# One run of 40 rows per image in the resident tile of a diagonal LSTM kernel

## The chip, the cores and the metric

The kernel runs on one core of a Trainium2 chip. The metric is device time in microseconds (us) of one execution. The core has TensorE (PE in the profile; PEld is its weight load), VectorE (DVE), ScalarE (ACT), GpSimd (POOL) and SyncE (SP), each with its own instruction queue, and 16 DMA engines.

## The reference, cut to what matters

The input `x` holds 16 images of 128 channels and 64 x 64 pixels in float32. Two layers follow each other, each of the form x + f(groupnorm(x)) with 32 groups of 4 channels. In layer 0, f is an LSTM that runs along the diagonals of the image. Each row of the image is shifted right by its own number, so that a step of the recurrence takes all rows at once, one column each:

```python
xs = skew(x)                       # row i shifted right by i
i_s = einsum('oi,bihw->bohw', w_is, xs) + b_is
def step((h, c), ist):             # over the 127 columns of the skewed image
    h_shift = pad(h)[:, :, :-1]    # the row above
    gates = ist + w_ss[:, :, 0] @ h_shift + w_ss[:, :, 1] @ h + b_ss
    o, f, i = sigmoid(gates[:, :384]) in three parts; g = tanh(gates[:, 384:])
    c = f * c + i * g
    h = o * tanh(c)
x = x + unskew(hs)                 # after _gn(x) on the way in
...
xq = xf @ pre_w.T + pre_b          # layer 1, for each pixel: 128 -> 4
z = _simulate(xq, q_weights)       # a circuit of 4 qubits
x = x + z @ post_w.T + post_b      # 4 -> 128
```

## The kernel before, in words

Channels lie on the 128 partitions. **Stage one** loads all images and takes their statistics. The tile `ring` (L110) stays in SBUF through the whole kernel and has room for 40 of the 64 rows of every image. It is cut into 10 blocks of 4 rows; the block is the outer dimension, then the image, then the 256 values of the 4 rows. So one image's 40 rows lie in ten runs of 1 KB per partition, and one block of all 16 images is one contiguous run. `block(r)` (L136) gives the index of the block that holds row r: rows 0 to 31 lie in blocks 2 to 9, rows 32 to 39 in blocks 0 and 1. `rows(b)` (L244) loads an image in five DMAs of two blocks on SP's queue; `behind(b)` (L252) brings the other 24 rows into small tiles, for the statistics alone. `statistics(b, k)` (L282) is a `bn_stats` on DVE for each 8 rows. Beside it `inv_step` (L187) runs the recurrence of a padding state on PE, ACT and POOL.

**Stage two** is the scan (`step`, L758), 160 steps in an order written out by hand. The rows are worked in two bands of 32 slots: while the first band's last rows finish, the second band's first rows begin, a slot for each row modulo 32. In a step the active slots of all 16 images lie side by side, row pairs in two halves (`q` = 0 and 1). The diagonal of a band is what the active slots read and write in `ring`: one pixel from each row, one column further to the left in each following row. `diagonal(t, band, q, j0, j1)` (L533) gives it in pieces, since rows of one block stand 64 values apart and the blocks 4096: single slots at odd ends, and runs of pairs as one access of four dimensions.

The order of the issue in a step t is:

- `differences` (L615): one subtraction on DVE (L617), and one or two on POOL (L620, L623); PE's products read them.
- `statistics(us)` (L708): on DVE, as many waiting `bn_stats` (L720) for layer 1's norm as fit in the time given. When a block of 4 rows of all 16 images is through, and its rows are among the first 24, the function issues the refill on SP's queue (L727): rows 40 and up of `x` into the same block, 2 MB.
- `residual(t - 1)` (L625): POOL adds the new h to the diagonal of the step before, band 0 and then band 1, `q` = 0 and then 1 (L632). When this completes a block of the first 24 rows, SP stores it to `low` in DRAM (L644), 2 MB. The statistics of that block follow in later steps.
- `normalised(t + 2)` (L561): POOL takes the diagonal of two steps ahead, subtracts the mean (L570) or the upper row (L575), and multiplies with 1/std (L580). PE's input product L589 reads it.
- PE's products with `wsT`, then `w1T` and `w0T` in turns (L768), gate by gate; `w0T` reads POOL's differences. DVE (L783, L835, L843, L846, L853) and ACT (L787, L818, L847) work out the gates and the new state. L853 writes the new h.
- PE's input product for step t + 1 (`gate_ps`, L582).
- POOL copies the last slot for the next band (`edge`, L873).

The tile framework finds which instruction has to wait for which from the address ranges of the accesses. In the scan the order of the instructions on each engine is as written (`manual_schedule`).

**Stage three** is layer 1, image by image: `angles`, `sines`, `squares`, `outputs`, and `finish` (L1057), which adds the result to x on DVE (L1072) and sends 256 KB to the output on SP's queue (L1073). The input is read from `ring`, and for the first 24 rows from tiles that are loaded from `low`. Because 8 rows of an image are two runs of 1 KB in `ring`, `finish` writes the sum to another place in the ring, two neighbouring images' places in a block, so that the DMA reads one run of 2 KB; these belong to images that are done with.

Of the kernel before, what the change touches and what calls it, by code (L numbers as in the profile page):

```python
# [11 lines left out]
F32 = mybir.dt.float32  # L12
# [69 lines left out]
def kernel(  # L82
# [24 lines left out]

    ring = const.tile([P, RING // ROWS, NB, BLOCK], F32, name="ring")  # L110
    NLOW = NH - RING
    NT = NLOW * NW // CHUNK
    low = dram.tile([NB, P, NLOW * NW], F32, name="low")
# [19 lines left out]
    w_out = const.tile([P, 128], F32, name="w_out")  # L133
    b_out = const.tile([P, 1], F32, name="b_out")

    def block(r):  # L136

        return (r + AHEAD if r < SLOTS else r - SLOTS) // ROWS

    def group_mean(psum, v, mean, which, scale):  # L140

# [15 lines left out]
    with ExitStack() as scan:  # L157
# [58 lines left out]
        with ExitStack() as prep:  # L216
# [25 lines left out]
            rests = {}  # L242

            def rows(b):  # L244
                for k in ORDERED:
                    at = (2 * k * ROWS - AHEAD) * NW if k else SLOTS * NW
                    nc.sync.dma_start(
                        out=ring[:, 2 * k : 2 * k + 2, b, :],
                        in_=xv[b, :, at : at + CHUNK].rearrange("c (k n) -> c k n", n=BLOCK),
                    )  # L250

            def behind(b):  # L252
# [27 lines left out]
            nc.gpsimd.memset(cinv[:, 0:1], 0.0)  # L280

            def statistics(b, k):  # L282
                v = ring[:, 2 * k : 2 * k + 2, b, :] if k < 5 else rests[b][k - 5]
                nc.vector.bn_stats(stats[:, b, k, :], v)

            def aggregated(b):
# [85 lines left out]
            for b in range(NB):  # L372
                while b < NB - 1 and done * (NB - 1) < EARLY * (b + 1):
                    inv_step(done, ps_inv)
                    keep(ps_keep, "keep", ring[:, 2, b, 0:P])
# [129 lines left out]
        origin = ring[:, 0, 0, 0:1]  # L505

        def active(t):
            return max(0, t - BAND - NW + 1), min(t + 1, SLOTS)
# [24 lines left out]
        def diagonal(t, band, q, j0, j1):  # L533


            j = j0
            while j < j1:
                odd = (j + AHEAD // 2 * (1 - band)) % 2
                n = 1 if odd or j + 1 == j1 else (j1 - j) // 2 * 2
                r = 2 * j + q + AHEAD * (1 - band)  # L540
                at = r // ROWS * NB * BLOCK + r % ROWS * NW + t - BAND * band - 2 * j - q
                dims = [[BLOCK, NB]]
                if n > 1:
                    dims = [[NB * BLOCK - ROWS, n // 2], [2 * NW - 2, 2]] + dims
                yield j, n, bass.AP(origin.tensor, origin.offset + at, [list(origin.ap[0])] + dims)
                j += n

        def slots(t, band):

            return max(0, t - BAND * band - NW + 1), min(SLOTS, t - BAND * band + 1)  # L550

        def over(v, n):
            if n == 1:
                return v
            return v.unsqueeze(1).unsqueeze(1).to_broadcast([P, n // 2, 2, NB])

        def by_pairs(v, q, j, n):
            v = v[:, q, j * NB : (j + n) * NB]
            return v if n == 1 else v.rearrange("p (k h i) -> p k h i", h=2, i=NB)

        def normalised(t):  # L561

            xn = xns[t % 2]
            for band in range(2):
                s0, s1 = slots(t, band)
                j0, j1 = max(0, s0 - 1 + s0 % 2) // 2, (s1 + 1) // 2
                for j, n, x0 in diagonal(t, band, 0, j0, j1):
                    nc.gpsimd.tensor_sub(by_pairs(xn, 0, j, n), x0, over(mean1, n))  # L570
                j0, j1 = s0 // 2, s1 // 2
                uppers = diagonal(t, band, 0, j0, j1)
                for (j, n, lower), (_, _, upper) in zip(diagonal(t, band, 1, j0, j1), uppers):
                    of = over(mean1, n) if plain(t) else upper
                    nc.gpsimd.tensor_sub(by_pairs(xn, 1, j, n), lower, of)  # L575
# [4 lines left out]
            nc.gpsimd.tensor_mul(v, v, r)  # L580
# [44 lines left out]
        def residual(t, new, engine=nc.gpsimd):  # L625

            for band in range(2):
                s0, s1 = slots(t, band)
                for q in range(2):
                    j0, j1 = (s0 + 1 - q) // 2, (s1 + 1 - q) // 2  # L630
                    for j, n, x1 in diagonal(t, band, q, j0, j1):
                        engine.tensor_add(x1, x1, by_pairs(new, q, j, n))  # L632
# [15 lines left out]


# [58 lines left out]
        def statistics(us):  # L708

            while waiting:  # L710
# [3 lines left out]
                    break  # L714
                waiting.pop(0)
                q = block(4 * g)
                v = ring[:, q, i, :].rearrange("p (r w) -> p r w", w=NW)[:, :, w0:w1]
                if w1 - w0 == NW:
                    v = ring[:, q, i, :]
                nc.vector.bn_stats(stats[:, i, g - FIRST * k, :], v)  # L720
                if i == NB - 1:
                    if g == FIRST - 1:
                        sums.append(early_sums())
                    elif g >= FIRST:
                        sums.append(late_sums(g, k, (w1 - w0) / NW))
                    if 4 * g < NLOW:
                        nc.sync.dma_start(  # L727
                            out=ring[:, q],
                            in_=xv[:, :, (RING + 4 * g) * NW : (RING + 4 * g + 4) * NW].rearrange(
                                "b c n -> c b n"  # L730
                            ),
                        )
# [143 lines left out]
        def low_rows(queue, n, v):  # L876
            b, k = n // NT, n % NT
            of = low[b, :, k * CHUNK : (k + 1) * CHUNK]
            queue.dma_start(out=v, in_=of if len(v.shape) == 2 else of.rearrange("p (k n) -> p k n", n=BLOCK))

        waiting = []
        begin(nc.gpsimd.tensor_copy, cst, 0, cinv, 0)
# [1 line left out]
        with tc.manual_schedule():  # L884
# [23 lines left out]
                add(ps[:, 1], by_one, inner[:, :, h])  # L908
            fill(1)

            v = ring[:, block(NH - ROWS)].rearrange("p i (r w) -> p i r w", w=NW)[:, :, :, NW - STRIP :]
# [64 lines left out]
    def rows_of(b, k):  # L976
        if k < NT:
            return lows[NT * b + k]
        q = block(2 * ROWS * k)
        return ring[:, q : q + 2, b, :]  # L980

    def half(v, c):

        if c is None:
            return v
        return v[:, c] if len(v.shape) == 3 else v[:, c * BLOCK : (c + 1) * BLOCK]

    def bank(pool, name):
        return pool.tile([P, CHUNK], F32, name=name, tag=pool.name)
# [67 lines left out]
    def finish(b, h, po, c=None):  # L1057
        for j in range(4):
            k = 4 * h + j
            v = rows_of(b, k)  # L1060
            x1, y, o = half(v, c), po[j], ov[b, :, k * CHUNK : (k + 1) * CHUNK]
            to = place = v
            if c is not None:
                o, to = o[:, c * BLOCK : (c + 1) * BLOCK], x1
            elif k >= NT:


                q = block(2 * ROWS * k)
                to = ring[:, q, b - 1 : b + 1, :] if b % 2 else ring[:, q + 1, b - 2 : b, :]
                y = y.rearrange("p (k n) -> p k n", n=BLOCK)  # L1070
                place = to.rearrange("p k n -> p (k n)")
            nc.vector.scalar_tensor_tensor(to, y, b_out, x1, ALU.add, ALU.add)  # L1072
            nc.sync.dma_start(out=o, in_=to if c is not None else place)  # L1073
            if c is None or c == 1 and k < NT:
                places.append(place)

    def idle():

# [93 lines left out]
```

## Time and profile before

Three runs took 1411.84, 1413.09 and 1413.08 us, a median of 1413.08. The profile shows one more execution. The page gives its span, and no separate total time for it.

| | |
|---|---|
| span of the profiled execution | 1411.1 us |
| median of the runs shown | 1413.08 us |
| busy: PE, DVE, POOL, ACT | 96%, 69%, 65%, 55% of the span |
| ring loads in stage one | 80 of 256 KB, median 5.6 us to landing |
| stores to `low`, refills | 6 and 6, of 2 MB each, medians 7.5 and 8.3 us |
| POOL's adds to `ring` (L632) | 487, 247.7 us |
| bytes moved by DMA | 107.06 MB |

Times are microseconds unless marked ns. A row of the slices shows the span in 40 parts; a digit is the busy share in tenths. For PEclk it is the clock that PE was granted, in tenths of full speed. A row of the costly groups names line, engine and operation, output and inputs with their shape, the count, then the busy time and the mean ns of one, then the engine's idle time just before, and what ended most of it. A row of the timeline is the start, the duration, the engine, the line and the operation; in brackets the idle time before it and what ended it. A DMA's row gives its issue; the time to landing counts from there.

### The profile page before, as it was taken

How to read it: one execution, taken by the hardware profiler on the slowest of the kernel's cores; microseconds unless marked ns; L12 is line 12 of the kernel's file. 1: busy time of each engine (PE TensorE's matmuls, PEld its weight loads, DVE VectorE, ACT ScalarE, POOL GpSimd, SP SyncE). 2: the span in 40 equal slices, each digit the busy share in tenths (PEclk: the TensorE clock that was granted, in tenths of full speed). 3: DMA queues.
4: the chain of work that ended last, by engine and by line, in shares of the span. 5: the costliest groups of instructions: out<-in, count | busy, mean ns of one | idle time of the engine just before them, and what ended most of it. 6: DMA issues, size and time to landing. Idle time of an engine off the chain costs nothing. (4 is left out here: it accounts for less than half of the span.)

```text
span 1411.1 us, 20316 instructions
## 1 busy us (share of the span) xinstructions
PE 1354.3 (96%) x6046; PEld 966.1 (68%) x6046; DVE 979.7 (69%) x2541; ACT 777.0 (55%) x1852; POOL 921.1 (65%) x1823
## 2 busy tenths in 40 slices
PE   6778999999999999999999999999999999999995
PEld 4658988777777777666677777776666777886332
DVE  7983565566665666787777776666665566876996
ACT  4545666555555555555555555555555566554331
POOL 4226788777777777777788876777777677773300
PEclk9999999999999999999999999999999999999997
DMA  9980000000000000133333100000000000004999
GB/s 326 367 287 2 1 2 0 1 1 1 0 1 1 0 1 1 60 120 120 120 120 120 60 1 1 0 1 1 1 1 0 1 1 1 2 30 143 386 404 350
DMA packets 78925, 107.06 MB, mean 76 GB/s; under 512 B 5552, under 2 KB 53712, under 8 KB 78816
## 3 DMA queue, kind: packets, MB, share of 16 engines
q1 hardware_dynamic: 74176, 94.39, 19.2%
q0 software_dynamic: 3408, 10.58, 2.0%
q8 instruction: 48, 0.79, 0.2%
q10 hardware_dynamic: 1232, 0.80, 0.2%
q14 instruction: 61, 0.50, 0.1%
HBM read 59.61 MB, written 46.14 MB: 75 GB/s over the span
## 5 line engine op out<-in xcount | busy, mean ns | idle before, releaser
L589 PE MATMUL ps<-spare,wxT 128*128 128x512 f32 (+18 forms) x1280 | 480.6, 519 | 0.0
L783 DVE TENSOR_TENSOR ps<-ps,both 128x256 f32<-128x256 f32 (+9 forms) x536 | 219.5, 411 | 304.4 <-PE ps L768 302.6
L787 ACT ACTIVATE ps<-ps,bias 128x512 f32<-128x512 f32 (+23 forms) x480 | 279.4, 583 | 221.7 <-DVE ps L783 185.2
L768 PE MATMUL ps<-spare,w1T 128*128 128x256 f32 (+16 forms) x1272 | 346.6, 354 | 8.8 <-DVE spare L744 4.6
L589 PEld LDWEIGHTS ps<-spare,wxT 128*128 128x128 f32 x1280 | 231.8, 191 | 172.6 <-issue 155.5
L768 PE MATMUL ps<-spare,w0T 128*128 128x256 f32 (+16 forms) x1272 | 343.8, 352 | 0.8 <-POOL spare L623 0.8
L818 ACT COPY both<-ps 128x256 f32<-128x256 f32 (+9 forms) x536 | 189.8, 356 | 181.1 <-PE ps L768 161.4
L632 POOL TENSOR_TENSOR ring<-ring,spare 128x256 f32<-128x256 f32 (+8 forms) x487 | 247.7, 540 | 30.8 <-DVE stats L720 20.7
L768 PEld LDWEIGHTS ps<-spare,w1T 128*128 128x128 f32 x1272 | 230.4, 190 | 35.8 <-DVE spare L853 6.8
L768 PEld LDWEIGHTS ps<-spare,wsT 128*128 128x128 f32 x1088 | 195.5, 190 | 80.5 <-DVE spare L853 29.9
L768 PE MATMUL ps<-spare,wsT 128*128 128x256 f32 (+14 forms) x1088 | 243.8, 366 | 2.4 <-DVE spare L853 1.2
L768 PEld LDWEIGHTS ps<-spare,w0T 128*128 128x128 f32 x1272 | 230.3, 190 | 22.2 <-POOL spare L623 1.0
L580 POOL TENSOR_TENSOR spare<-spare,rstd 128x512 f32<-128x512 f32 (+10 forms) x160 | 171.0, 1069 | 14.8 <-DVE rstd L154 2.3
L575 POOL TENSOR_TENSOR spare<-ring 128x256 f32<-128x256 f32 (+8 forms) x213 | 147.2, 701 | 0.0
L847 ACT ACTIVATE g<-cst 128x256 f32<-128x256 f32 (+20 forms) x320 | 103.2, 369 | 64.2 <-DVE cst L846 63.3
L570 POOL TENSOR_TENSOR spare<-ring,mean 128x16 f32<-128x16 f32 (+8 forms) x247 | 130.9, 540 | 8.3 <-DVE mean L144 7.2
L853 DVE TENSOR_TENSOR spare<-g,ps 128x256 f32<-128x256 f32 (+17 forms) x319 | 105.7, 368 | 43.3 <-ACT g L847 40.8
L623 POOL TENSOR_TENSOR spare<-spare 128x240 f32<-128x240 f32 (+9 forms) x136 | 102.7, 755 | 29.3 <-DVE spare L853 25.5
L787 ACT ACTIVATE g<-ps,bias 128x512 f32<-128x512 f32 (+20 forms) x160 | 97.4, 609 | 26.9 <-DVE ps L783 20.7
L873 POOL COPY spare<-spare 128x16 f32<-128x16 f32 x64 | 21.1, 330 | 134.2 <-DVE spare L853 134.2
L846 DVE TENSOR_TENSOR cst<-cst,ps 128x256 f32<-128x256 f32 (+20 forms) x320 | 104.6, 368 | 5.5
L843 DVE TENSOR_TENSOR ps<-ps,g 128x512 f32<-128x512 f32 (+20 forms) x160 | 95.1, 595 | 19.0 <-ACT g L787 18.8
(370 smaller groups left out, 1097.3 us busy)
## 6 DMA issues: line engine op xcount, KB each, us to landing
out_dram<-ring SPq DMA_DIRECT2D x93, 256.0 KB, 5.3
ring<-in_x_dram SPq DMA_DIRECT2D x80, 256.0 KB, 5.6
low<-ring SPq DMA_DIRECT2D x6, 2048.0 KB, 7.5
ring<-in_x_dram SPq DMA_DIRECT2D x6, 2048.0 KB, 8.3
spare<-in_x_dram SPq DMA_DIRECT2D x27, 256.0 KB, 5.5
rest<-in_x_dram SPq DMA_DIRECT2D x21, 256.0 KB, 5.6
ring<-low POOLq DMA_DIRECT2D x18, 256.0 KB, 6.7
low<-low POOLq DMA_DIRECT2D x14, 256.0 KB, 5.9
```

What stands on the lines that cost most here:

```text
L570: nc.gpsimd.tensor_sub(by_pairs(xn, 0, j, n), x0, over(mean1, n))
L575: nc.gpsimd.tensor_sub(by_pairs(xn, 1, j, n), lower, of)
L580: nc.gpsimd.tensor_mul(v, v, r)
L589: nc.tensor.matmul(ps[g][:, :, a:b], lhsT=wxT[:, g * 128 : (g + 1) * 128], rhs=xns[t % 2][:, :, a:b], start=t > 0, stop=True, skip_group_c ...
L632: engine.tensor_add(x1, x1, by_pairs(new, q, j, n))
L768: nc.tensor.matmul(out, lhsT=w[:, g * 128 : (g + 1) * 128], rhs=rhs, start=False, stop=True, skip_group_check=True,)
L783: nc.vector.tensor_add(v, v, both[g][:, a:b])
L787: nc.scalar.activation(to[:, :, a:w], ps[g][:, :, a:w], FUNC[g], bias=bias[:, g : g + 1])
L818: nc.scalar.copy(both[g][:, a:b], ps[g][:, 0, a:b])
L846: nc.vector.tensor_add(c[:, q], c[:, q], ig[:, q])
L847: nc.scalar.activation(th[:, q, a:w], c[:, q], AF.Tanh)
L853: nc.vector.tensor_mul(new[:, q, a:v], th[:, q, a:v], act[GO][:, q, a:v])
```

## The change

`ring` gets the image as its outer dimension, and each image's 40 rows in one run of 10 KB per partition. `place(r)` is the offset of row r in it, and `block(r)` now gives an access: 4 rows of all 16 images, 16 runs of 1 KB that stand 10 KB apart. A diagonal is then regular from row to row (63 values further for each row, 126 for each pair), so `diagonal` gives a single access of pairs by images, and `residual` and `normalised` issue one instruction where they issued one for each piece. `rows` loads an image in three DMAs: 16 rows, 16 rows, and 8 rows. `finish` writes in place. Refill and store keep their position in the issue order, and what they move.

```diff
-    ring = const.tile([P, RING // ROWS, NB, BLOCK], F32, name="ring")
+    ring = const.tile([P, NB, RING * NW], F32, name="ring")
...
+    def place(r):
+        return (r + AHEAD if r < SLOTS else r - SLOTS) * NW
     def block(r):
-        return (r + AHEAD if r < SLOTS else r - SLOTS) // ROWS
+        return ring[:, :, place(r) : place(r) + BLOCK]
...
             def rows(b):
-                for k in ORDERED:
-                    at = (2 * k * ROWS - AHEAD) * NW if k else SLOTS * NW
+                for r, n in ((0, SLOTS // 2), (SLOTS // 2, SLOTS // 2), (SLOTS, AHEAD)):
                     nc.sync.dma_start(
-                        out=ring[:, 2 * k : 2 * k + 2, b, :],
-                        in_=xv[b, :, at : at + CHUNK].rearrange("c (k n) -> c k n", n=BLOCK),
+                        out=ring[:, b, place(r) : place(r) + n * NW],
+                        in_=xv[b, :, r * NW : (r + n) * NW],
                     )
...
         def diagonal(t, band, q, j0, j1):
-            j = j0
-            while j < j1:
-                odd = (j + AHEAD // 2 * (1 - band)) % 2
-                n = 1 if odd or j + 1 == j1 else (j1 - j) // 2 * 2
-                r = 2 * j + q + AHEAD * (1 - band)
-                at = r // ROWS * NB * BLOCK + r % ROWS * NW + t - BAND * band - 2 * j - q
-                dims = [[BLOCK, NB]]
-                if n > 1:
-                    dims = [[NB * BLOCK - ROWS, n // 2], [2 * NW - 2, 2]] + dims
-                yield j, n, bass.AP(origin.tensor, origin.offset + at, [list(origin.ap[0])] + dims)
-                j += n
+            r = 2 * j0 + q + AHEAD * (1 - band)
+            at = r * NW + t - BAND * band - 2 * j0 - q
+            dims = [[2 * NW - 2, j1 - j0], [RING * NW, NB]]
+            return bass.AP(origin.tensor, origin.offset + at, [list(origin.ap[0])] + dims)
...
                     j0, j1 = (s0 + 1 - q) // 2, (s1 + 1 - q) // 2
-                    for j, n, x1 in diagonal(t, band, q, j0, j1):
-                        engine.tensor_add(x1, x1, by_pairs(new, q, j, n))
+                    if j0 < j1:
+                        x1 = diagonal(t, band, q, j0, j1)
+                        engine.tensor_add(x1, x1, by_pairs(new, q, j0, j1))
...
                             out=low[:, :, 4 * g * NW : (4 * g + 4) * NW].rearrange("b c n -> c b n"),
-                            in_=ring[:, block(4 * g)],
+                            in_=block(4 * g),
...
                 q = block(4 * g)
-                v = ring[:, q, i, :].rearrange("p (r w) -> p r w", w=NW)[:, :, w0:w1]
+                v = q[:, i].rearrange("p (r w) -> p r w", w=NW)[:, :, w0:w1]
...
-                            out=ring[:, q],
+                            out=q,
...
-            to = place = v
+            to = v
...
-            elif k >= NT:
-                q = block(2 * ROWS * k)
-                to = ring[:, q, b - 1 : b + 1, :] if b % 2 else ring[:, q + 1, b - 2 : b, :]
-                y = y.rearrange("p (k n) -> p k n", n=BLOCK)
-                place = to.rearrange("p k n -> p (k n)")
             nc.vector.scalar_tensor_tensor(to, y, b_out, x1, ALU.add, ALU.add)
-            nc.sync.dma_start(out=o, in_=to if c is not None else place)
+            nc.sync.dma_start(out=o, in_=to)
```

The remaining edits follow the new shape: `normalised` loops over no pieces, `statistics` of stage one, `rows_of`, `half` and the strip of the last block read the same elements by the new offsets.

More of the change, by code (lines that the diff above doesn't have):

```diff
@@ L282, in statistics @@
             def statistics(b, k):
-                v = ring[:, 2 * k : 2 * k + 2, b, :] if k < 5 else rests[b][k - 5]
+                v = ring[:, b, k * CHUNK : (k + 1) * CHUNK] if k < 5 else rests[b][k - 5]
                 nc.vector.bn_stats(stats[:, b, k, :], v)
@@ L374 @@
                     inv_step(done, ps_inv)
-                    keep(ps_keep, "keep", ring[:, 2, b, 0:P])
+                    keep(ps_keep, "keep", ring[:, b, CHUNK : CHUNK + P])
                     keep(ps_keep, "keep", wsT[:, 0:P])
@@ L504 @@
         nc.vector.memset(cst[:, :, 0:LEAST], 0.0)
-        origin = ring[:, 0, 0, 0:1]
+        origin = ring[:, 0, 0:1]
         def active(t):
@@ L552, in over, with by_pairs @@
         def over(v, n):
[L553 to L559, printed above, removed]
+            return v.unsqueeze(1).to_broadcast([P, n, NB])
+        def by_pairs(v, q, j0, j1):
+            return v[:, q, j0 * NB : j1 * NB].rearrange("p (j i) -> p j i", i=NB)
         def normalised(t):
@@ L568, in normalised @@
                 j0, j1 = max(0, s0 - 1 + s0 % 2) // 2, (s1 + 1) // 2
-                for j, n, x0 in diagonal(t, band, 0, j0, j1):
-                    nc.gpsimd.tensor_sub(by_pairs(xn, 0, j, n), x0, over(mean1, n))
+                if j0 < j1:
+                    x0 = diagonal(t, band, 0, j0, j1)
+                    nc.gpsimd.tensor_sub(by_pairs(xn, 0, j0, j1), x0, over(mean1, j1 - j0))
                 j0, j1 = s0 // 2, s1 // 2
[L572 to L575, printed above, removed]
+                if j0 < j1:
+                    lower, upper = (diagonal(t, band, q, j0, j1) for q in (1, 0))
+                    of = over(mean1, j1 - j0) if plain(t) else upper
+                    nc.gpsimd.tensor_sub(by_pairs(xn, 1, j0, j1), lower, of)
             a, b = columns(t)
@@ L630, in residual @@
                     j0, j1 = (s0 + 1 - q) // 2, (s1 + 1 - q) // 2
-                    for j, n, x1 in diagonal(t, band, q, j0, j1):
-                        engine.tensor_add(x1, x1, by_pairs(new, q, j, n))
+                    if j0 < j1:
+                        x1 = diagonal(t, band, q, j0, j1)
+                        engine.tensor_add(x1, x1, by_pairs(new, q, j0, j1))
             for g in range(NG2):
@@ L716, in statistics @@
                 q = block(4 * g)
-                v = ring[:, q, i, :].rearrange("p (r w) -> p r w", w=NW)[:, :, w0:w1]
+                v = q[:, i].rearrange("p (r w) -> p r w", w=NW)[:, :, w0:w1]
                 if w1 - w0 == NW:
-                    v = ring[:, q, i, :]
+                    v = q[:, i]
                 nc.vector.bn_stats(stats[:, i, g - FIRST * k, :], v)
@@ L878, in low_rows @@
             of = low[b, :, k * CHUNK : (k + 1) * CHUNK]
-            queue.dma_start(out=v, in_=of if len(v.shape) == 2 else of.rearrange("p (k n) -> p k n", n=BLOCK))
+            queue.dma_start(out=v, in_=of)
         waiting = []
@@ L909 @@
             fill(1)
-            v = ring[:, block(NH - ROWS)].rearrange("p i (r w) -> p i r w", w=NW)[:, :, :, NW - STRIP :]
+            v = block(NH - ROWS).rearrange("p i (r w) -> p i r w", w=NW)[:, :, :, NW - STRIP :]
             d, sq = (work.tile([P, NB, ROWS, STRIP], F32, name=f"strip{i}", tag=f"both{i}") for i in range(2))
@@ L978, in rows_of @@
             return lows[NT * b + k]
-        q = block(2 * ROWS * k)
-        return ring[:, q : q + 2, b, :]
+        at = place(2 * ROWS * k)
+        return ring[:, b, at : at + CHUNK]
     def half(v, c):
@@ L985, in half @@
             return v
-        return v[:, c] if len(v.shape) == 3 else v[:, c * BLOCK : (c + 1) * BLOCK]
+        return v[:, c * BLOCK : (c + 1) * BLOCK]
     def bank(pool, name):
@@ L1061, in finish @@
             x1, y, o = half(v, c), po[j], ov[b, :, k * CHUNK : (k + 1) * CHUNK]
-            to = place = v
+            to = v
             if c is not None:
                 o, to = o[:, c * BLOCK : (c + 1) * BLOCK], x1
-            elif k >= NT:
-                q = block(2 * ROWS * k)
-                to = ring[:, q, b - 1 : b + 1, :] if b % 2 else ring[:, q + 1, b - 2 : b, :]
-                y = y.rearrange("p (k n) -> p k n", n=BLOCK)
-                place = to.rearrange("p k n -> p (k n)")
             nc.vector.scalar_tensor_tensor(to, y, b_out, x1, ALU.add, ALU.add)
-            nc.sync.dma_start(out=o, in_=to if c is not None else place)
+            nc.sync.dma_start(out=o, in_=to)
             if c is None or c == 1 and k < NT:
-                places.append(place)
+                places.append(v)
     def idle():
```

## The prediction

> **What bounds the kernel now.** I read the page from the top: busy shares, slices, costly groups, DMA issues; then the timeline of the one step around the first refill, where the change touches what is late.
>
> ```profile
> PE 1354.3 (96%) x6046; PEld 966.1 (68%) x6046; DVE 979.7 (69%) x2541; ACT 777.0 (55%) x1852; POOL 921.1 (65%) x1823
> ...
> PE   6778999999999999999999999999999999999995
> ...
> POOL 4226788777777777777788876777777677773300
> PEclk9999999999999999999999999999999999999997
> DMA  9980000000000000133333100000000000004999
> ```
>
> Three stages show. In slices 1 to 3 (to about 100 us) the DMA row is full: images load while DVE takes statistics. From 108 to 1283 us PE stands at 9 throughout: the scan. In the last four slices DMA is full again: layer 1 writes out. The scan is 83% of the span and PE has no gaps in it; POOL at 7 or 8 is no bound, it waits for DVE once a step. In the middle the DMA row shows six exchanges of ring rows (store to `low`, refill from `in_x`).
>
> ```profile
> L632 POOL TENSOR_TENSOR ring<-ring,spare 128x256 f32<-128x256 f32 (+8 forms) x487 | 247.7, 540 | 30.8 <-DVE stats L720 20.7
> ...
> L873 POOL COPY spare<-spare 128x16 f32<-128x16 f32 x64 | 21.1, 330 | 134.2 <-DVE spare L853 134.2
> ...
> low<-ring SPq DMA_DIRECT2D x6, 2048.0 KB, 7.5
> ring<-in_x_dram SPq DMA_DIRECT2D x6, 2048.0 KB, 8.3
> ```
>
> The residual add L632 never waits for a DMA, though each refill takes 8.3 us to land. L873 idles 134.2 us over 64 steps, 2.1 us a step: POOL's slack. The timeline of POOL, SP and PE in step 70, where the first refill is issued:
>
> ```profile
> 610.46 0.86 POOL L623 TENSOR_TENSOR spare<-spare 128x240 f32<-128x240 f32 x1
> 611.29 2.34 POOL L632 TENSOR_TENSOR ring<-ring,spare 128x16 f32<-128x16 f32 x7
> 613.59 0.67 POOL L570 TENSOR_TENSOR spare<-ring,mean 128x192 f32<-128x192 f32 x1
> ...
> 615.82 1.27 POOL L580 TENSOR_TENSOR spare<-spare,rstd 128x512 f32<-128x512 f32 x1
> 618.73 0.20 POOL L873 COPY spare<-spare 128x16 f32<-128x16 f32 x1 [1.64 <-DVE spare L853]
> 618.88 0.41 POOL L620 TENSOR_TENSOR spare<-spare,spare 128x16 f32<-128x16 f32 x1
> 619.25 0.69 POOL L623 TENSOR_TENSOR spare<-spare 128x240 f32<-128x240 f32 x1
> ```
>
> ```profile
> 613.59 0.38 SPq L727 DMA_DIRECT2D ring<-in_x_dram  x1
> ```
>
> ```profile
> 621.07 0.59 PE L768 MATMUL ps<-spare,w0T 128*128 128x256 f32 x2
> ```
>
> POOL's order in a step is edge copy, differences for PE, residual, then the normalised diagonal of two steps ahead. The differences end at 619.94 (619.25 + 0.69) and PE's w0T product wants them at 621.07: 1.13 us to spare. The refill is issued at 613.59 and lands at 621.9, when the residual of its own step is long over.
>
> **What the Trainium skill says.** "TensorE: Matmul & The Clock Gate", Part 1: after an idle window of about 3.4 us PE falls to half clock, and regains the full one after about 3.4 us of work. The trace agrees with the half and with the recovery, and is harsher on the idle. Windows (times, total, then PE, PEld, DVE, ACT, POOL busy, granted clock, DMA share, GB/s):
>
> ```profile
> 100.00:101.00 1.00, 0.03 (x1) 0.06 (x1) 0.83 (x2) 0.00 (x0) 0.00 (x0) 1.00 0.00 0
> 103.00:104.00 1.00, 1.00 (x3) 0.48 (x2) 0.78 (x4) 0.98 (x2) 0.00 (x0) 0.50 0.00 0
> ```
>
> PE is idle for some 1.4 us to 101, and from 103 to about 106.4 runs at 0.50. "DMA: Bandwidth & Descriptors" gives one load stream with 4 KiB rows 408.7 GB/s (section on the iDMA fabric); the load phase here, with 1 KB rows in part, shows 362 to 374. "GPSIMD Engine Reference", section 3.1, gives about 2.6 cycles an element plus a dispatch of each instruction; L632's forms agree (256 elements 862 ns, 16 elements 229 ns: 2.6 ns an element and about 0.19 us fixed).
>
> **The change, part by part.**
>
> *Loads.* 80 ring loads become 48, with runs of 4 and 2 KB in place of 1 KB. All loads are 33.6 MB (16 images of 2 MB); at 408.7 instead of 368 GB/s the 21 MB of the ring would take 51.3 instead of 57 us, 5.7 less. But DVE is as full: L284's 128 statistics of 694 ns are 88.8 us, from 13.4 to 100.5, with only 9.4 us of waits for ring loads. The inverse-state chain ends at 94.3, so little more than 5 us can come out of both. Against it: the first load is twice as large, so DVE starts later by up to 1 us, and the weights on ACT's queue share engines with bigger packets. Between −4 and +3; I take −1. At nothing stands SP's shorter issue time, behind loads that fill the engines.
>
> *POOL.* The diagonals become one access each: in the built order L570 falls from 247 to 191 instructions, L575 from 244 to 188, the residual from 487 to 375. That is 224 fewer, each with 0.19 to 0.23 us fixed, 43 to 51 us of POOL. PE covers all of it, since POOL waits 2.1 us a step for DVE: 0. The stride over images becomes 10 KB; no row shows that. Today's strided L632 and contiguous L623 cost the same per element (862 for 256, 801 for 240), so I take no change. It could cost at most what the idle covers without effect; the case beyond is a rival.
>
> *New waits.* A diagonal was several accesses, each within a 4-row block that lay by itself. Now the block of 4 rows (`block`) is a stripe through every image, and a diagonal is one access across many rows and all images. Its address range overlaps that of the block in transfer, although no element is shared, and the built program orders them: the first residual add waits, in six steps, for the refill that the same step's statistics have just sent off, and in six others for the store of the step before. The kernel before has no such wait; there POOL meets the refill only in later steps, when it has landed.
>
> Refill, six times. Behind the waiting add in POOL's queue lie the other residual adds, the normalised diagonal (SP only issues, at 613.59), the next edge copy and the next differences, for which PE's w0T waits. First one: landing 613.59 + 8.3 = 621.9; then residual in fewer pieces 1.9 (the four-piece one at 593.19 took 1.91), normalised 3.5 (613.59 to 617.09), copy and differences 1.2: ready at 628.5 instead of the wanted 621.07, **7.4 us**. The others are issued at 647.27 to 785.08, with w0T wanted 8.95 us later (656.22; the last 794.03): 8.3 + 1.9 + 3.5 + 1.2 − 8.95 = 5.95 each, five times 29.8. Sum **37 us**. PE is the bound in every step around, so nothing makes it up. Ends: an 8.1 or 8.6 landing, shorter late diagonals (the adds shrink to under 10 slots in the band that waits): 30 to 42.
>
> Clock. Each of these stops leaves PE idle 6 to 7 us, so I expect 3.4 us at half clock after it: 1.7 us lost, six times, **10 us**; ends 0 and 20 (the whole recovery counted twice).
>
> Store, six times. It lands 7.5 us after issue (585.55 → 593.1), before the last statistics of that step (596.6), for which the residual now waits as well. That holds POOL 1.7 to 3.5 us; idle of 1.4 to 2.4, pieces saved (0.4 to 1.0) and the 1.13 spare cover it: 0, ends 0 and +4. Statistics wait for POOL in some more places; DVE has idle time every step (L783 302.6 us before it): 0.
>
> *Layer 1 in place.* The writes go out in 2 KB runs either way, DMA at 386 to 404 GB/s sets its end: 0, with L1072's waits for the shifted places gone, and no more than 1 us.
>
> Sum against the profiled execution: 1411.1 − 1 + 37 + 10 = 1457. The page gives its span alone; the runs shown have a median of 1413.08, 2.0 above. So 1459 us.
>
> **Rivals.**
>
> 1. *No clock drop.* The stops happen, but the clock stays: 1459 − 10 = 1449. For it: the stop is short against a step. Against: the 0.50 at 103.
>
> 2. *The wait is covered, the loads win* (the other side). Each add waits at the head of POOL's queue, but the refill is already there when POOL comes to it, because statistics and refill run ahead of the residual; then the load phase's gain of up to 4 is left: 1409 to 1413 on the runs' scale, mostly within reach of faster. It decides the sign where the landing comes within 8.95 − 6.6 = 2.3 us of the issue (0.9 for the first): what PE's need leaves after POOL's 6.6 us of work behind the wait. Against: 8.1 us is the shortest landing of the six, and DVE sends the refill 2.3 us after POOL could begin its residual (611.29 to 613.59).
>
> 3. *POOL becomes the bound.* A full step's ring accesses on POOL are two residual adds of 0.86, L570 0.85 and L575 1.08, 3.65 us; with L580, copy and differences, 2.5 more, it is 6.1 of the step's 8.6. If the 10 KB stride slowed ring accesses by 70%, POOL would fill the step; at twice their time it stands 1.1 us over it, in some 100 steps 110 us: with the stops about 1570. For it: no row has that stride; against: strided and contiguous run alike now.
>
> 4. *The packets do nothing*: DVE sets the load phase and the −1 goes: 1460, within the forecast's spread.
>
> **Chances.** Stops with clock loss 0.66, without 0.20, POOL bound 0.06, covered 0.08. The last is faster (0.06) or the same (0.02). 0.2%, 2.8 us, is about what a measurement here can tell from no change. Range: the low end from rival 1 with the small stops and the good loads (1413 − 4 + 30 = 1439), the high end from the stops' upper end with a clock loss of 20 and the store's 4 (1413 + 3 + 42 + 20 + 4 = 1482). What is left out is the covered case and a slow POOL.
>
> **What would show it.** The waits list should hold POOL's residual waiting for DMA ring<-in_x six times, some 8 to 10 us each, and PE's w0T waiting for POOL's differences six times, about 6 us. Slices 18 to 23 should lose PE's 9 and some of PEclk's. POOL's instruction count should fall by 224 and its busy time by about 45 us; ring loads should number 48. The scan outside 615 to 800 us should keep 8.6 us steps. I am wrong if POOL's residual waits for no DMA; if PE stays full in the middle; or if steps far from the refills grow longer, which means POOL's access rate.

## The result and the profile after

The changed kernel takes 1460.66 us (median of 4 runs, 1459.45 to 1460.85) against 1412.82 us before: ratio 1.0341, interval 1.0327 to 1.0356. The forecast was 1459, slower. The profiled execution has a span of 1458.5 us, 47.4 over the one of before. The page of the kernel after, with the rows that answer to those shown ahead:

```profile
PE 1368.0 (94%) x6046; PEld 974.5 (67%) x6046; DVE 972.0 (67%) x2541; ACT 776.8 (53%) x1852; POOL 887.0 (61%) x1599
...
PE   6788999999999999988888899999999999999995
...
POOL 4226777776677767566556577777777666763310
PEclk9999999999999999999999999999999999999998
DMA  9950000000000000323332200000000000003999
...
L627 POOL TENSOR_TENSOR ring<-ring,spare 128x256 f32<-128x256 f32 (+15 forms) x375 | 231.7, 645 | 103.8 <-DMA ring<-in_x_dram 56.2
...
low<-ring SPq DMA_DIRECT2D x6, 2048.0 KB, 7.5
ring<-in_x_dram SPq DMA_DIRECT2D x6, 2048.0 KB, 8.1
```

PE falls from 9 to 8 in six slices, the ones in which the refills run; elsewhere in the scan it stands as before. POOL has 224 instructions and 34 us of work less, and PE gained nothing by it. L627, the residual, now idles 56.2 us for refills. The waits (engine, line, releaser: us in total, times, longest us) give the two ends of the chain:

```profile
POOL ring L627 <- DMA ring<-in_x_dram: 56.2, 6, 10.0
...
PE ps L763 <- POOL spare L617: 35.1, 7, 6.6
```

Six waits of 9.4 us on POOL become six stops of PE. Here is the first of them in the timeline, on SP, POOL and PE:

```profile
611.14 0.37 SPq L722 DMA_DIRECT2D ring<-in_x_dram  x1
```

```profile
619.53 1.89 POOL L627 TENSOR_TENSOR ring<-ring,spare 128x208 f32<-128x208 f32 x4 [10.04 <-DMA ring<-in_x_dram]
621.38 0.67 POOL L564 TENSOR_TENSOR spare<-ring,mean 128x192 f32<-128x192 f32 x1
...
623.56 1.26 POOL L574 TENSOR_TENSOR spare<-spare,rstd 128x512 f32<-128x512 f32 x1
...
625.10 0.69 POOL L617 TENSOR_TENSOR spare<-spare 128x240 f32<-128x240 f32 x1
```

```profile
618.65 0.59 PE L763 MATMUL ps<-spare,w1T 128*128 128x256 f32 x2
625.84 0.80 PE L763 MATMUL ps<-spare,w0T 128*128 128x256 f32 x1 [6.60 <-POOL spare L617]
```

This refill lands 8.3 us after its issue (the median of the six is 8.1), POOL works off what lay behind the wait for 6.3 us (619.53 to 625.79), and w0T starts at once. After it PE is slow. Windows of the kernel after (columns as ahead):

```profile
622.00:624.00 2.00, 0.00 (x0) 0.00 (x0) 0.00 (x0) 0.00 (x0) 1.92 (x5) 0.59 0.00 0
...
626.00:628.00 2.00, 2.00 (x5) 1.64 (x6) 0.43 (x1) 0.36 (x1) 2.00 (x5) 0.50 0.00 0
...
630.00:632.00 2.00, 2.00 (x8) 1.21 (x7) 1.96 (x4) 1.29 (x3) 1.07 (x1) 1.00 1.05 348
```

The clock falls while PE stands still and is back by 630. In windows of 0.5 us around all six stops, the time of low clock is 3.4 us once and 6.8 us five times, part of it inside the stop; what PE loses while it works is 1.7 to 3.0 us a stop, 13.5 in all. Waiting 34.5 and clock 13.5 make 48.0 of the loss; step by step the stops shift the scan by 49.3 us, so 1.3 us, some 0.2 a stop, are in neither. In these two executions the scan starts 1.3 to 1.7 us earlier than before. That gain is not a fixed amount: the profiled execution of before had half clock from 102.97 to 106.38, and among the eight profiled executions that load and start the scan as the change does the first input product starts between 103.1 and 104.4 us, against 104.5 and 104.6 in two with that of before.

### The profile page after: what moved, and what is told of

Same layout as the page of the kernel before. It is cut to its first block, busy times and chain, and to the rows that moved or that the text cites. A ratio compares the mean times of both kernels' runs of the same rounds, so it can differ in the third digit from the quotient of the medians.

```text
span 1458.5 us, 20029 instructions
## 1 busy us (share of the span) xinstructions
PE 1368.0 (94%) x6046; PEld 974.5 (67%) x6046; DVE 972.0 (67%) x2541; ACT 776.8 (53%) x1852; POOL 887.0 (61%) x1599
## 4 chain that ended last, share of the span: by engine, by line
PE 77%; DVE 4%; DMA 3%; POOL 3%; issue 1%; ACT 1%; DVEq 0%; ACTq 0%; SPq 0%; POOLq 0%
PE ps L763 44%; PE ps L583 26%; DMA ring<-in_x_dram 3%; PE po_None L1042 3%; PE theta_None L991 2%; PE am_None L1020 1%; POOL ring L627 1%; DVE spare L848 1%; DVE stats L715 1%; DVE ps L838 1%; POOL spare L574 1%; DVE ps L778 1%; POOL spare L569 1%; DVE cst L841 0%; ACT g L842 0%
## 5 line engine op out<-in xcount | busy, mean ns | idle before, releaser
L763 PE MATMUL ps<-spare,w0T 128*128 128x256 f32 (+16 forms) x1272 | 352.3, 359 | 35.1 <-POOL spare L617 35.1
L763 PE MATMUL ps<-spare,w1T 128*128 128x256 f32 (+16 forms) x1272 | 353.2, 360 | 9.4 <-DVE spare L739 5.0
L627 POOL TENSOR_TENSOR ring<-ring,spare 128x256 f32<-128x256 f32 (+15 forms) x375 | 231.7, 645 | 103.8 <-DMA ring<-in_x_dram 56.2
L763 PEld LDWEIGHTS ps<-spare,w0T 128*128 128x128 f32 x1272 | 234.8, 194 | 60.3 <-POOL spare L617 37.7
L763 PEld LDWEIGHTS ps<-spare,w1T 128*128 128x128 f32 x1272 | 234.8, 194 | 38.3 <-DVE spare L848 6.9
L569 POOL TENSOR_TENSOR spare<-ring 128x256 f32<-128x256 f32 (+13 forms) x165 | 140.1, 849 | 0.0
L564 POOL TENSOR_TENSOR spare<-ring,mean 128x256 f32<-128x256 f32 (+15 forms) x191 | 123.0, 644 | 5.6 <-DVE mean L148 5.4
L841 DVE TENSOR_TENSOR cst<-cst,ps 128x256 f32<-128x256 f32 (+20 forms) x320 | 104.6, 368 | 5.5
L830 DVE TENSOR_TENSOR cst<-cst,ps 128x512 f32<-128x512 f32 (+20 forms) x160 | 92.8, 580 | 16.4 <-POOL spare L607 10.8
```

The lines of the kernel that those rows point to most:

```text
L564: nc.gpsimd.tensor_sub(by_pairs(xn, 0, j0, j1), x0, over(mean1, j1 - j0))
L569: nc.gpsimd.tensor_sub(by_pairs(xn, 1, j0, j1), lower, of)
L627: engine.tensor_add(x1, x1, by_pairs(new, q, j0, j1))
L763: nc.tensor.matmul(out, lhsT=w[:, g * 128 : (g + 1) * 128], rhs=rhs, start=False, stop=True, skip_group_check=True,)
L841: nc.vector.tensor_add(c[:, q], c[:, q], ig[:, q])
```

## The experiments

The kernel before was run beside each of them; its medians were 1411.35 us with experiments 1 to 4, 1412.00 with 5, 6, 9 and 10, and 1411.64 with 7, 8 and 11. The ratios are to these.

**1. No refills.**

```diff
-                    if 4 * g < NLOW:
-                        nc.sync.dma_start(out=q, in_=xv[...])   # L722
```

> The changed kernel with the six refills left out, so rows 40 to 63 are worked on stale values; all else, the six waits for the stores and the extra waits for statistics among them, is as in the change. Theory (the stops come from the residual's wait for the refill, the rest of the layout costs nothing in the scan): all six stops and clock dips go, and what is left is the load phase's gain of 1.7 us and nothing else: 1410 to 1413 us, PE's wait for POOL's differences back under 2 us. Rival (the stripe layout costs by itself: the waits for stores and statistics, 10 KB strides on POOL): part of the 48 us stays, 1420 us or more.

1410.56 us, ratio 0.9991 (0.9983 to 1.0000). The waits list:

```profile
POOL ring L627 <- DVE stats L715: 42.4, 30, 3.3
...
PE ps L756 <- POOL spare L617: 0.6, 1, 0.6
```

POOL still waits for statistics, more often and longer than before (20.7 us, 19 times), and the store's order is still there; PE does not notice. So all of the loss hangs on the six refills. That it is the wait for them, and not the transfer, is left to experiments 2 and 4.

**2. The wait alone, in the kernel before.**

```diff
+            while refilled:                       # the refilled block's first element
+                nc.gpsimd.tensor_copy(seen, refilled.pop())
             if t:
                 residual(t - 1, now)
```

> The kernel before with one thing added: in the six steps that issue a refill, POOL copies one element of the refilled block into a spare tile ahead of the residual, so that it has to wait for the landing. Layout, diagonals in pieces and loads are those of before. Theory: the wait alone makes the loss: six stops of 6 to 7 us of PE plus 2 us of half clock each, a little more than in the change since residual and normalised take more pieces here (0.5 us): 1460 to 1466 us. Rival (the loss belongs to the layout or the single accesses): within 5 us of 1413.

1463.08 us, 1.0366 (1.0352 to 1.0380). The waits list:

```profile
POOL seen L811 <- DMA ring<-in_x_dram: 54.4, 6, 9.9
...
PE ps L771 <- POOL spare L623: 37.1, 7, 6.9
```

Old layout, old pieces, old loads, and the same two lines as in the change. The wait is enough for the loss.

**3. The residual in pieces on the new layout.**

```diff
-                        x1 = diagonal(t, band, q, j0, j1)
-                        engine.tensor_add(x1, x1, by_pairs(new, q, j0, j1))
+                    j = j0
+                    while j < j1:
+                        n = 1 if (j + AHEAD // 2 * (1 - band)) % 2 else min(2, j1 - j)
+                        x1 = diagonal(t, band, q, j, j + n)
+                        engine.tensor_add(x1, x1, by_pairs(new, q, j, j + n))
+                        j += n
```

> The changed kernel, with the residual's single access cut again at the borders of the 4-row blocks (one slot or one pair per instruction), on the new layout. Theory (it is the block's shape, a stripe through all images, that the ordering cannot tell from a diagonal; the single access is not needed for it): the waits stay and the time stays with them or grows by the extra instructions behind the landing, about 0.2 us for each of some 12 more: 1460 to 1478 us. Rival (the single access over many rows makes the overlap): the waits go, 1411 to 1415 us.

1480.80 us, 1.0486 (1.0470 to 1.0502), 3 us over the upper end given. These pieces are finer than those of before: 2111 residual adds instead of 487. The waits list:

```profile
POOL ring L629 <- DMA ring<-in_x_dram: 51.2, 6, 9.7
...
PE ps L766 <- POOL spare L617: 48.4, 12, 8.9
```

The single access is not what brings the order about: the block as a stripe through all images is enough. The added instructions lengthen what lies behind each landing.

**4. Each refill in two DMAs of two rows.**

```diff
-                        nc.sync.dma_start(out=q, in_=xv[... 4 rows ...])
+                        for r in range(4 * g, 4 * g + 4, 2):
+                            nc.sync.dma_start(
+                                out=ring[:, :, place(r) : place(r) + 2 * NW],
+                                in_=xv[:, :, (RING + r) * NW : (RING + r + 2) * NW].rearrange("b c n -> c b n"),
+                            )
```

> The changed kernel with each refill issued as two DMAs of two rows (1 MB each, runs of 512 bytes), at the same place of the order. As built, the residual then waits for none of them; only the normalised diagonal does, which reads the rows. Theory: the six stops are gone and the load phase's 1.7 us are kept: 1409 to 1413 us, a shade under before. Rival (the shorter runs land so late that the normalised diagonal waits for them, row 40 being wanted one step after the issue): landings over 10 us and stops of PE of a few us in the following step: 1420 us or more.

1410.38 us, 0.9993 (0.9986 to 0.9999). The waits list has no POOL wait for a ring refill; the residual's longest are these:

```profile
POOL ring L627 <- DVE stats L715: 42.4, 30, 3.3
POOL ring L627 <- DVE spare L849: 10.8, 7, 2.7
```

The refill is as large and in the same place, but the residual no longer waits for it: stripes half as wide are not taken to overlap the diagonal. The landings are later (6.5 to 10.0 us, median 9.4) and cost nothing, since only the normalised diagonals wait for them, and none of these is held up. Why the framework tells two rows from a diagonal and not four was not looked into.

**5. PE kept busy in the stops.**

```diff
                     half(g, 1, w1T, diff[:, 1])
+                    if g == ORDER[0]:             # in the step after a refill
+                        for _ in range(6 * busy):
+                            keep(ps_small, "small", wxT[:, 0:384])
```

> The changed kernel with six matmuls more (128x384, results unused, about 0.9 us each) in PE's queue in each step after a refill, between the first w1T and the first w0T product, where PE otherwise stands still for 5.4 to 6.6 us. The waits stay. Theory (the loss has two parts: 34.5 us of PE waiting and 13.5 us of half clock after it): the clock stays near full, the wait stays, and 12 to 14 us come back: 1446 to 1450 us. Rival (the slower products after a stop are no matter of PE's idle time): 1460 us as in the change.

1448.41 us, 1.0264 (1.0248 to 1.0280); the granted clock is 0.995 as before, against 0.982 in the change. POOL's wait is whole, PE's is filled:

```profile
POOL ring L627 <- DMA ring<-in_x_dram: 57.0, 6, 10.3
...
PE ps L765 <- POOL spare L617: 3.0, 5, 1.4
```

Against the kernel before the loss is 36.4 us instead of 47.8: 11.4 us come back by doing useless work. The two parts of the loss can be removed separately.

**6. Half a refill.**

```diff
-                            out=q, in_=xv[:, ...]
+                            out=q[:, 0:8], in_=xv[0:8, ...]
```

> The changed kernel with the refill of images 8 to 15 left out, so each refill moves 1 MB instead of 2 and these images' rows 40 to 63 are worked on stale values. Theory: the landing comes at about 5 us instead of 8.1, each stop is 3 us shorter (2.4 to 3.6 us), and the clock still falls after it, since 1.4 us of idle was enough at the scan's start: 1.7 us each; with no stops 1410.6, so 1410.6 + 6 x (2.8 + 1.7) = 1438 us, range 1430 to 1443. Rival (below an idle window of 3.4 us the clock stays): about 1427 us, granted clock as in the kernel before.

1412.36 us, 1.0002 (0.9994 to 1.0011): a miss for both theories. The waits list:

```profile
POOL ring L627 <- DMA ring<-in_x_dram: 11.6, 5, 2.8
...
PE ps L763 <- POOL spare L617: 0.6, 1, 0.6
```

The edit did two things. The landing came 5.3 us after the issue, as expected. But the issue moved too. It no longer stands behind the statistics of the last images and goes out right behind POOL's L569 (to 608.24); the first one and its wait:

```profile
608.27 0.37 SPq L722 DMA_DIRECT2D ring<-in_x_dram  x1
```

```profile
613.63 1.90 POOL L627 TENSOR_TENSOR ring<-ring,spare 128x208 f32<-128x208 f32 x4 [2.81 <-DMA ring<-in_x_dram]
```

In the change the first issue stands at 611.14, 2.9 us later; counted from the start of the input product just before it, which comes 1.3 us later in this run, the issue is 4.2 us earlier, and the other five are 4.0 earlier. So the data is there 1.1 to 1.4 us after the point at which the change issues. POOL waits in five steps. The first of the six steps becomes 1.0 us longer, the others do not: the landing came in time.

**7. The other half.** The same edit with images 8 to 15, so that the issue stays.

> The changed kernel with the refill of images 0 to 7 left out instead, whose rows 40 to 63 are then worked on stale values. Leaving out images 8 to 15 had also let the refill go 2.9 us earlier, since it no longer waited for the last images' statistics; here it waits for them as in the change, and only the size differs: landing 5.3 us after the issue instead of 8.1. The waits' theory: stops of 6.6 - 2.8 = 3.8 us once and 5.4 to 6.2 - 2.8 = 2.6 to 3.4 us five times, 18 us in all. If the clock falls after each of them (1.4 us of idle were enough at the scan's start): 1.7 to 2.3 us more each, 1438 to 1443 us in all. If it takes a full idle window of 3.4 us: 1427 to 1431 us, with one dip at most.

1433.33 us, 1.0158 (1.0144 to 1.0171), between the two cases. Two windows after PE's stops, the first after the stop of 3.83 us, the second after the next one, of 2.77:

```profile
626.00:628.00 2.00, 2.00 (x6) 1.64 (x5) 0.43 (x1) 0.83 (x2) 2.00 (x5) 0.50 0.49 170
```

```profile
664.00:666.00 2.00, 2.00 (x11) 1.74 (x11) 0.86 (x2) 0.80 (x2) 2.00 (x5) 1.00 0.00 0
```

In the profiled execution the clock fell once, after 3.83 us. After the five stops of 2.60 to 2.85 us it did not. The stops have the expected size, and each of the five shifts the scan by 0.3 to 0.5 us more than the wait shown, which is most of the difference to 1427 to 1431. That the five left the clock alone is no rule of their length. The slowest of the four executions, 1436.78 us, shows a clock of 0.991 where the others show 0.994, which is some 9 us more at half clock (0.003 of 1435 us, doubled), wherever these lay; and in the profiled one each of the five stops lay across a border between two of the stretches of 3.41 us by which the clock changes (last section).

**8. The refill behind the normalised diagonal.**

```diff
             if t + 2 < NSTEP:
                 normalised(t + 2)
+            refill()                              # L722, taken out of statistics()
```

> The changed kernel with the 2 MB refill issued after the step's residual and normalised diagonal; the waiting residual is then that of the next step. Theory (what counts is the landing against PE's need, not that there is a wait): issue some 2 us before the next step's copy and differences, landing 8.1 us later, then 6.7 us of POOL's work, against a w0T that is wanted a step (8.6 us) later than in the change: stops of about 2 us instead of 5.4 to 6.6, 12 us in all, with or without a clock dip (0 to 10): 1420 to 1433 us. Rival (any wait for a landing in POOL's queue costs its stop): near 1460.

1423.82 us, 1.0089 (1.0074 to 1.0105). The waits list:

```profile
POOL ring L627 <- DMA ring<-in_x_dram: 27.5, 6, 5.4
...
PE ps L769 <- POOL spare L617: 9.7, 11, 2.0
```

The residual waits in six steps as in the change, for half the time, and PE stands 9.7 us in pieces of 2.0 and less, with no dip of the clock. What counts is when the landing comes against PE's need.

**9. Loads of 8 rows.** The change's ring loads, in smaller pieces:

```diff
-                for r, n in ((0, SLOTS // 2), (SLOTS // 2, SLOTS // 2), (SLOTS, AHEAD)):
+                for r, n in ((0, 8), (8, 8), (16, 8), (24, 8), (32, 8)):
```

> The changed kernel with the ring loaded in five DMAs of 8 rows an image, runs of 2 KB, in place of three with runs of 4 and 2 KB. The question is what ended DVE's statistics at 94.2 us instead of 100.9. If fewer and larger packets did (DVE's bn_stats average 676 instead of 692 ns, and DMA moves 406 GB/s instead of 370): the statistics end between, at 95 to 98 us, with bn_stats at 680 to 690 ns. If the contiguous place in SBUF did, whatever the packets: 94 to 95 us as in the change. The total is 1460 us either way, the scan starting at 103 to 104 us, since PE's mean waits behind fillers to 99.7.

A single run, 1458.90 us. The statistics, with the last aggregate, end at 96.9 us, between 100.9 before and 94.2 after; the nine profiled executions with the change's load stage end at 94.1 to 95.8, so 96.9 is outside their spread. From 15 to 90 us DMA moves 369 GB/s before, 390 here, and 400 after (391 to 400 in the nine), which by itself tells 390 from the change hardly at all. DVE's instructions tell more. The median `bn_stats` on the ring is 694 ns before and 676 in both kernels of the new layout; on the other tiles, which the layout does not touch, it is 694 before and here, and 675 to 677 with the 4 KB runs. These records overlap with their neighbours' and hide most of the difference: from one start to the next the median on the ring is 664 ns before, 593 here and 593 after; on the other tiles it is 666 to 687, 633 to 651, and 593. DVE's busy time up to the last aggregate is 89.5, 85.9 and 83.8 us. So the packets have a share, since only they differ from the change. That the place in SBUF has one too is likely from the ring's instructions, but it is not shown apart from the step from 1 to 2 KB runs. The input product starts at 104.3 us, within the spread of 103.1 to 104.4 of those that start the scan alike.

**10. The mean early.** Refills as in 4, and at the end of the load stage:

```diff
-            for v in (rests[NB - 2][0], rests[NB - 2][2], rests[NB - 1][0]):
-                keep(ps_small, "small", v[:, 0 : 3 * P])
+            group_mean(ps_small, mv1[:, :, 0], mean1, 1, 1.0)   # ahead of the first products
...
-            keep(ps_gate, "gate", wxT[:, 0 : 3 * P])
+            # the first w1T and w0T products: two gates here, two behind gv
```

> Refills in two DMAs of two rows, and at the end of the load stage PE's three filler matmuls on the last loads are taken out and the group mean is issued ahead of the first recurrent products, which fill the time in which DVE works on the variance. In the change the statistics end at 94.2 us and PE takes up the mean at 99.7. Theory (the loads' gain of 6.7 us was lost behind PE's queue): the mean runs at about 95 us, the first input product 3.5 us later instead of 103.2: 4 to 5 us less than with the two refills alone, 1404 to 1408 us. Rival (PE has more gaps and loses its clock there, or DVE's statistics become later when PE no longer waits): 1409 to 1412 us.

1405.72 us, 0.9956 (0.9944 to 0.9969): 6.3 us under the kernel before. In the changed kernel DVE's last aggregate and PE's mean stand thus:

```profile
93.80 0.37 DVE L290 BATCH_NORM_AGGREGATE mv<-stats 128x2 f32<-128x48 f32 x1
```

```profile
99.69 0.40 PE L147 MATMUL gm<-mv,wide_sb 128*128 128x16 f32 x2
```

With the early mean the aggregate ends at 94.84, and PE's row is:

```profile
94.90 0.39 PE L147 MATMUL gm<-mv,wide_sb 128*128 128x16 f32 x2 [0.43 <-ACT hinv L210]
```

The first input product moves from 103.2 to 98.5 us.

**11. The mean early, in the kernel before.** The same edit on the old layout and loads.

> The kernel before, layout and loads untouched, with the early mean's edit at the end of the load stage (no three fillers, group mean ahead of the first products). Here the statistics end at 100.9 us and PE's mean runs at 101.0. Theory (the 5 to 6 us that the early mean gave on the new layout are the loads' gain set free): nothing to set free here, 1410 to 1413 us, same as before. Rival (the shorter order itself saves the time): 1405 to 1408 us.

1414.52 us, 1.0019 (1.0012 to 1.0027): 2.9 us more, where no change was expected. PE's mean, and a window after it:

```profile
100.78 0.61 PE L143 MATMUL gm<-mv,wide_sb 128*128 128x16 f32 x2 [6.09 <-DVE mv L287]
```

```profile
103.00:104.00 1.00, 1.00 (x7) 1.00 (x6) 0.17 (x1) 0.22 (x1) 0.00 (x0) 0.50 0.00 0
```

Here the statistics end at 100.7, PE waits for them 6.09 us without the fillers, and then runs the first products at half clock, from 99.03 to 105.86; the fillers had kept PE busy over that wait. The mean runs no earlier than before (100.78 against 100.97), so the edit has nothing to set free here, and its gain on the new layout is the loads'. A saving by the shorter order itself could hide behind the half clock, but no more than the 2.5 us that PE lost in it.

## Why the prediction was right, point by point

**The wait.** Right in place, count and size: six waits of the residual for the refill of its own step, and behind them in POOL's queue the normalised diagonal, the copy and the differences. Experiment 4, which keeps the transfers, shows the wait to be necessary for the loss, experiment 2 sufficient; experiment 1 leaves nothing to the rest of the layout. The prediction laid the overlap to two things together, the block as a stripe and the access across many rows; experiment 3 shows that the first alone does it, and experiment 4 that half the stripe's width undoes it.

**37 us of stops.** Measured 34.5. The first was given as 7.4 and is 6.6, the others 5.95 and are 5.4 to 6.2. The landing was taken as 8.3; it is 8.3 for the first and 8.1 in the median. POOL's work behind it was taken as 6.6 and is 6.3, and PE stood still 8.1 us after the first issue instead of 7.5.

**10 us of clock.** Measured 13.5 in the records, and 11.4 came back in experiment 5. The mis-sized term is the 1.7 us a stop: it held the recovery to one stretch of 3.4 us with PE at work, but five of the six dips are twice as long and in some of them up to 3.0 us were lost. The row of PEclk, which the prediction expected to lose some of its 9s, kept them all: a dip of 6.8 us takes less than a tenth from a slice of 36 us.

The reading that 1.4 us of idle are enough does not hold as a rule: it rested on one dip after such a gap at the scan's start, and in experiment 2 the same gap of 1.37 us, at 99.73, has no dip behind it. A need for 3.4 us of idle does not hold either. The Trainium skill ("TensorE: Matmul & The Clock Gate", Part 1) has PE fall to half clock after an idle window of about 3.4 us. The traces here agree with the length of the window, 3.41 us, and not with its being idle: in the change the window ahead of one of the six falls had PE busy for 0.39 of it.

**−1 for the loads.** About right in sum (experiments 1 and 4 stand 0.8 and 1.0 us under before, the scan starts 1.3 to 1.7 earlier), and wrong in what limits it. The step that failed is "little more than 5 us can come out of both": the statistics ended 6.7 us earlier, and 5.7 of these are DVE's own busy time, 89.5 us before and 83.8 after, which the prediction held fixed at 128 times 694 ns. (The first statistics start at 5.0 us, not at 13.4, and the records overlap.) Most of the gain was then lost in PE's queue, where three fillers stood ahead of the mean to 99.7. The prediction saw the inverse-state chain's end at 94.3 as a limit and did not look at the fillers behind it. Experiment 10 moves the first input product 4.7 us forward, and with experiment 11 this is the lost gain, within the reserve named there.

**At nothing: POOL's fewer pieces, the store's wait, statistics, layer 1.** Experiment 1 has all of them and stands at 0.9991. POOL's saving was 34 us instead of 43 to 51, under PE's cover. The ring accesses' rate did not change with the 10 KB stride: 861 ns for 256 elements, 862 before. Steps away from the refills take 8.62 us before and after. That closes rival 3. One reading in the prediction is wrong. It has L632's 2.6 ns an element agree with the Trainium skill ("GPSIMD Engine Reference", section 3.1), but the section gives 2.6 cycles, which at the 1.2 GHz that it uses are 2.2 ns (an estimate from its figures). The two agree in their digits alone; the prediction counted with the measured time, so no term of it is touched.

**The rivals.** Rival 1, no clock drop, is the state that experiment 5 made by hand. Rival 2, a covered wait, is what experiment 6 shows by accident, with the landing early enough. The prediction had put the point at 0.9 us after the issue for the first and 2.3 for the others. Counted from the change's time of issue the data was there after 1.1 us the first time, in a step that became 1.0 us longer, and after 1.2 to 1.4 the other times, which cost nothing. The change lands at 8.1. Rival 4 is out as a mechanism: the packets do work, but the time lay behind another queue. In the total it cannot be told from the forecast.

**The sum.** 1459 was given and 1460.66 measured. The terms are further off than the sum: the stops were put 2.5 us too high, the clock 3.5 too low, and 1.3 of the shift stand in no term. That these nearly cancel is luck; that stops and clock are the two terms is not.

## What to carry to other kernels

When a layout changes, list for each in-flight transfer which accesses the framework now orders behind it: two patterns that share no element can still be ordered, and one transfer in two narrower ones, or a later place in the queue, can take away all or most of the cost. Price such a wait by the landing, plus the work queued behind the waiting instruction, minus the time until the bound engine needs it; add the clock for stops of more than about 2 us, and count on it from about 4 (estimates from these traces, in the next section). And a stage that ends earlier gives nothing until what follows it in every in-order queue, fillers included, has been moved up too.

## What the runs showed of the hardware

Within each trace of this case the granted clock of PE falls and rises on a grid of 3.41 us, whose place differs from run to run. The dips in the middle of the kernels last one, two or three of its stretches: 3.41, 6.83, and in experiments 2 and 3 also 10.24 us. How much of one stretch PE was busy, by its records, tells the clock of the next in all but two cases. From 60 us on, up to the last stage, over all 13 runs:

| clock in a stretch | PE busy in it | clock in the next |
|---|---|---|
| full | 0.39 or less, 26 stretches | half, every time |
| full | 0.43 or more, all others | full, but for two, at 0.54 and 0.55 |
| half | 0.82 or less, 26 stretches | half, every time |
| half | 0.89 or more, 28 stretches | full, every time |

The two exceptions, one of them at the scan's start in the kernel before, each hold a gap of 1.37 us between short matmuls; why the clock fell there stays open. The table explains experiment 7: the stop of 3.83 us left PE busy for 0.16 of a stretch, and each of the five shorter ones was shared by two stretches, the emptier of which was still busy for 0.45 to 0.59. From the limits 0.39 and 0.43 follows an estimate for a PE that is otherwise full: a stop under 1.9 us leaves the clock alone, one over 4.2 us always brings it down, and between them it depends on where the stop falls on the grid. A dip takes a second stretch where the stop leaves PE busy for 0.82 or less of the first.

DVE's `bn_stats` of 512 elements, done while loads fill the DMA engines, had medians of 694 ns with 1 KB runs and 675 to 677 with 4 KB runs, and from one start to the next 664 to 687 and 593. Experiment 9 gives the loads' packets a share in this; by what means they act, no run here shows.
